# Joining the block inverses of two heads at once on four row groups of TensorE

## The chip, the cores and the metric

The kernel runs on one core of a Trainium2 chip. The core has TensorE (matrix products, here PE), VectorE (DVE), ScalarE (ACT), GpSimd (POOL), SyncE (SP, which here only issues transfers) and sixteen DMA engines. The metric is device time in microseconds, from the first to the last instruction. The profiler records one execution; its span is used to read where the time goes.

## The reference

The program is one transformer block with adaptive layer norms: a gated linear attention with a delta rule, then a feed-forward part whose hidden values are thinned two out of four. All data are fp32. The part that matters here is the recurrence of the attention, for 8 sequences of 256 tokens, 16 key heads with two value heads each, all of width 128:

```python
def step(S, inp):
    q_t, k_t, v_t, b_t, d_t = inp
    Sk = jnp.einsum('bhi,bhipj->bhpj', k_t, S)
    dv = b_t[..., None] * (v_t - Sk)
    upd = jnp.einsum('bhi,bhpj->bhipj', k_t, dv)
    S = S * d_t[:, :, None, :, None] + upd
    o = jnp.einsum('bhi,bhipj->bhpj', q_t, S)
    return (S, o)
```

Over a chunk of 128 tokens this is the solution of a triangular system. The kernel forms the triangular 128x128 matrix of each chunk, inverts it, and applies the inverse by matrix products.

## The kernel before, in words

The sequences are taken in four pairs, and the key heads in groups of four (`GH`), so that there are 16 groups and 64 turns of one "head" (a key head for a pair of sequences). A head has 8 triangular matrices: two sequences, two chunks, two value heads.

While one group is attended, the next is prepared in the background (`ahead`). `stage_a` projects and convolves the keys, makes the products of keys with decays (tile `a_t`) and writes the diagonal 32x32 blocks of each triangle to a scratch in DRAM. `stage_b` reads the 128 blocks of the group back with one block a partition, inverts them all at once on VectorE, and writes the inverses to DRAM in two orientations (`scr_x`, `scr_y`).

`levels` joins these inverses for one head. It reads the inverse blocks into `x_even`, `x_top` and the diagonal of `t_inv`, and then goes through four steps with a `yield` after each. Step one multiplies 32x32 blocks below the diagonal by inverse blocks (line 703, tile `ps_w`), and ScalarE copies the result (711, 712). Step two multiplies from the other side (line 717, `ps_t`); VectorE transposes one half (725) and ScalarE writes the joint 64x64 inverses to `t_inv` and `x_top` (729, 732, 738), of which a transfer moves a part to other partitions (730, `low_up`). Steps three and four do the same with 64x64 blocks (743 and 746, copy 750; 754 and 757, copies 760 and 761). In the 32-wide steps the blocks stand on partitions 0 to 31 and 64 to 95 (step one) or 32 to 63 and 96 to 127 (step two), so that successive products alternate between two of the array's four row groups. In the 64-wide steps they alternate between the two halves.

`attend` uses the finished inverse `t_inv` (lines 810 and 853) for one sequence of the head. There are two `t_inv` tiles: one is read for the head that is attended while the other is written for the next.

The main loop at the end goes through the heads. For each it makes a list of turns: the attention of two sequences, the join (`levels`) for the head that comes next, the projections for the next head, the output products of an earlier one. It takes one step of each turn in rotation, and after each rotation a measured amount of background work (`along`). This gives the order in which the program is written; a scheduler then places the instructions of each engine by its own estimates, so that the order within an engine is not quite that of the loop. All transfers are issued by SP and ACT; those of the joins are on SP, in order with the loads of decays (`dbc`), of the feed-forward weights (`w_ff`, `w_dn`) and the scratch traffic.

Of the kernel before, what the change touches and what calls it, by code (L numbers as in the profile page):

```python
# [18 lines left out]
P = 128  # L19
# [29 lines left out]
def adaln_block(  # L49
# [316 lines left out]
    with ExitStack() as scope:  # L366
# [45 lines left out]
        t_inv = [single.tile([P, 2 * NS, P], F32, name=f"t_inv{i}") for i in range(2)]  # L412
        x_top = single.tile([P, NS, 2 * Q], F32, name="x_top")
# [260 lines left out]
        def levels(rec, scr_x, scr_y, tt):  # L674

            hp = rec["hp"]
            xv = scr_x.rearrange("(g s q) a b -> g q a s b", g=GH, q=NQ)
            yv = scr_y.rearrange("(g s q) a b -> g q a s b", g=GH, q=NQ)
            a_f = rec["a"].rearrange("p i s t -> p (i s) t")
            NP = 2 * NS  # L680

            x_even = single.tile([P, NP, Q], F32, name="x_even")
            low_up = single.tile([P, NS, 2 * Q], F32, name="low_up")
            for q in (0, 2):
                nc.sync.dma_start(out=x_even[q * Q : (q + 1) * Q], in_=xv[hp, q])
            for q in (1, 3, 0, 2):
                rows = slice(q * Q, (q + 1) * Q)
                nc.sync.dma_start(out=tt[rows, :, rows], in_=yv[hp, q])  # L690
                if q < 2:
                    for i in range(2):
                        nc.sync.dma_start(
                            out=x_top[i * 2 * Q + q * Q : i * 2 * Q + (q + 1) * Q, :, rows],
                            in_=xv[hp, q, :, i * NS : (i + 1) * NS],
                        )
            nc.sync.dma_start(out=low_up[2 * Q :], in_=a_f[0 : 2 * Q, NS:, 2 * Q :])
            even = [slice(0, Q), slice(2 * Q, 3 * Q)]
            odd = [slice(Q, 2 * Q), slice(3 * Q, P)]
            ps = bank(ps_inv, [P, NP, Q], "ps_w")  # L700
            for s in range(NP):
                for h in range(2):
                    nc.tensor.matmul(
                        ps[odd[h], s, :],
                        lhsT=a_f[even[h], s, odd[h]],
                        rhs=x_even[even[h], s, :],
                        start=True,
                        stop=True,
                    )
            w1 = single.tile([P, NP, Q], F32, name="w1")  # L710
            nc.scalar.copy(w1[odd[0]], ps[odd[0]])
            nc.scalar.copy(w1[odd[1]], ps[odd[1]])
            yield
            ps = bank(ps_inv, [P, NP, Q], "ps_t")
            for s in range(NP):
                for h in range(2):
                    nc.tensor.matmul(
                        ps[even[h], s, :],
                        lhsT=w1[odd[h], s, :],
                        rhs=tt[odd[h], s, odd[h]],  # L720
                        start=True,
                        stop=True,
                    )
            low = mixp.tile([Q, NP, Q], F32, tag="low", name="low", bufs=1)
            nc.vector.transpose(
                low.rearrange("p s t -> p (s t)"),
                ps[even[0]].rearrange("p s t -> p (s t)"),
            )
            nc.scalar.activation(tt[even[1], :, odd[1]], ps[even[1]], AF.Copy, scale=-1.0)
            nc.sync.dma_start(out=low_up[0 : 2 * Q], in_=tt[2 * Q :, NS:, 2 * Q :])  # L730
            for i in range(2):
                nc.scalar.activation(
                    x_top[i * 2 * Q + Q : (i + 1) * 2 * Q, :, 0:Q],
                    low[:, i * NS : (i + 1) * NS],
                    AF.Copy,
                    scale=-1.0,
                )
            nc.scalar.activation(tt[even[0], :, odd[0]], ps[even[0]], AF.Copy, scale=-1.0)
            yield
            top, bottom = slice(0, 2 * Q), slice(2 * Q, P)  # L740
            ps = bank(ps_inv, [P, NS, 2 * Q], "ps_w2")
# [479 lines left out]
```

## Time and profile before

| | |
|---|---|
| three runs | 2126.72, 2133.49, 2134.71 us |
| median | 2133.49 us |
| span of the profiled execution | 2126.1 us |
| granted TensorE clock, mean | 0.988 |
| TensorE idle in the span | 72 us |
| 32-wide products, lines 703 and 717: records, busy | 4096, 102.0 us |
| 64-wide products, lines 743, 746, 754, 757: records, busy | 2048, 181.7 us |
| bytes moved over the span | 226.85 MB, mean 107 GB/s |

The profiled execution's own time is known by its span alone, which lies near the fastest of the three runs and 7.4 us below their median. "Busy" counts the time in which at least one record of a group is open; for short products on TensorE a record stays open far longer than it keeps the next from starting, so distances between starts say more. A line such as `L703 PE MATMUL ps_w<-x_even,a_t 32*32 32x32 f32 x2048 | 53.7, 194 | 7.0` gives the source line, the engine, the tile written and the tiles read, the shape, the number of records, the busy time in us, the mean of one record in ns, and the engine's idle time just before such records.

### The profile page before, as it was taken

Reading aid. Unit: us, or ns where it says so; the run is one execution under the profiler, and the core shown is the slowest. Engines: PE = TensorE matmul, PEld = TensorE weight load, DVE = VectorE, ACT = ScalarE, POOL = GpSimd, SP = SyncE. Lnnn points to the kernel's source line nnn. Section 1 sums busy time; section 2 is a strip of 40 time slices with the busy share of each in tenths; the row PEclk is TensorE's granted clock in tenths of the full one; section 3 lists DMA queues with packets and bytes.
Section 4 is the critical chain, followed back from the end, with each engine's and each line's share of the span. In section 5 each row is a group of like instructions: output and inputs, shape, how many; then the busy total and the mean of one; then the engine's idle time right before and its main releaser. Section 6 shows DMA issues by size and latency. Waiting matters only on the chain.

```text
span 2126.1 us, 46444 instructions
## 1 busy us (share of the span) xinstructions
PE 2054.1 (97%) x16684; PEld 1633.6 (77%) x16684; DVE 1660.8 (78%) x4039; ACT 1356.1 (64%) x4579; POOL 367.8 (17%) x375
## 2 busy tenths in 40 slices
PE   8989999999999999999999999999999999999998
PEld 5567777777777787778778687778778778787887
DVE  6788787878879587897878779787896958879357
ACT  3577767776766467576576666667666656666552
POOL 3121202112120111212021020211112011120010
PEclk9999999999999999999999999999999999999999
DMA  4342424233242443434343343443434244343236
GB/s 135 98 112 69 113 66 118 79 78 113 82 116 82 124 118 92 124 97 120 115 103 102 117 117 104 113 118 98 121 98 120 67 124 129 96 114 96 73 90 216
DMA packets 324517, 226.85 MB, mean 107 GB/s; under 512 B 254520, under 2 KB 266168, under 8 KB 324288
## 3 DMA queue, kind: packets, MB, share of 16 engines
q1 hardware_dynamic: 304416, 163.34, 28.8%
q10 hardware_dynamic: 19872, 60.54, 9.1%
q8 instruction: 133, 2.18, 0.4%
q14 instruction: 96, 0.79, 0.1%
HBM read 186.28 MB, written 29.12 MB: 101 GB/s over the span
## 4 chain that ended last, share of the span: by engine, by line
PE 66%; DVE 13%; DMA 7%; ACT 6%; issue 2%; SPq 1%; POOL 1%; ACTq 0%; DVEq 0%; POOLq 0%
PE ps_qv L432 10%; PE ps_y L907 9%; PE ps_z L646 8%; PE ps_ks L818 5%; PE ps_ff L190 4%; PE ps_k L432 3%; DVE cv L420 3%; PE ps_u L853 2%; PE ps_out L244 2%; PE ps_o L837 2%; PE ps_kk L532 2%; PE ps_gt L893 2%; PE ps_o L859 2%; DMA blk<-scr 2%; PE ps_u L810 2%
## 5 line engine op out<-in xcount | busy, mean ns | idle before, releaser
L420 DVE SCALAR_TENSOR_TENSOR cv<-ps_qv,conv_sb,cv 128x510 f32<-128x510 f32 (+1 forms) x564 | 410.0, 736 | 43.4 <-ACT cv L418 41.5
L432 PE MATMUL ps_qv<-h_bp,wh 128*128 128x512 f32 x768 | 367.3, 602 | 3.0 <-DVE cv L420 2.0
L105 POOL TENSOR_TENSOR rs<-ss,minus_halves 128x4 f32<-128x4 f32 x128 | 133.2, 1049 | 1040.8 <-DVE ss L864 1023.7
L646 PE MATMUL ps_z<-wh,h_bp 128*128 128x256 f32 x1024 | 249.9, 386 | 12.1 <-ACT gz L653 11.3
L907 PE MATMUL ps_y<-wo,og_p 128*128 128x256 f32 x1024 | 236.0, 380 | 0.9 <-DVE cv L420 0.9
L646 PEld LDWEIGHTS ps_z<-wh,h_bp 128*128 128x128 f32 x1024 | 186.3, 192 | 39.8 <-ACT gz L653 12.4
L432 PEld LDWEIGHTS ps_qv<-h_bp,wh 128*128 128x128 f32 x768 | 133.3, 192 | 105.4 <-issue 97.8
L418 ACT ACTIVATE cv<-ps_qv,conv_sb 128x512 f32<-128x512 f32 x188 | 129.3, 690 | 122.3 <-PE ps_qv L432 121.9
L907 PEld LDWEIGHTS ps_y<-wo,og_p 128*128 128x128 f32 x1024 | 188.0, 190 | 23.7 <-DVE cv L420 1.4
L604 DVE TENSOR_TENSOR tmp<-blk 128x30 f32<-128x30 f32 (+14 forms) x480 | 157.1, 327 | 46.8 <-DMA blk<-scr 37.6
L516 POOL TENSOR_TENSOR diag<-consts,bk 128x1032 f32<-128x1032 f32 x64 | 122.8, 1918 | 371.6 <-DVE bk L507 371.6
L844 ACT ACTIVATE junk<-o 128x128 f32<-128x128 f32 x512 | 154.1, 305 | 42.9 <-DVE o L860 36.4
L551 DVE TENSOR_TENSOR_SCAN e<-dbc,diag 128x1032 f32<-128x1032 f32 x60 | 137.9, 2299 | 47.6 <-POOL diag L516 46.3
L610 DVE TENSOR_TENSOR blk<-blk,tmp 128x30 f32<-128x30 f32 (+14 forms) x480 | 156.9, 327 | 9.6
L420 DVE SCALAR_TENSOR_TENSOR k_t<-ps_k,conv_sb,k_t 128x510 f32<-128x510 f32 (+1 forms) x189 | 139.2, 738 | 22.0 <-ACT k_t L418 20.3
L877 DVE SCALAR_TENSOR_TENSOR og<-o,rs,gz 128x128 f32<-128x128 f32 x512 | 143.9, 345 | 14.1 <-POOL rs L105 14.0
L818 PE MATMUL ps_ks<-u,cross 128*128 128x128 f32 x1024 | 144.7, 284 | 2.8 <-DVE aq L800 1.5
L784 ACT ACTIVATE vn<-ps_v,nk 128x256 f32<-128x256 f32 x256 | 105.7, 482 | 62.0 <-PE ps_v L779 61.2
L818 PEld LDWEIGHTS ps_ks<-u,cross 128*128 128x128 f32 x1024 | 133.7, 197 | 12.5 <-ACT u L812 5.3
L190 PE MATMUL ps_ff<-h,w_ff 128*128 128x128 f32 x1024 | 130.5, 277 | 3.3 <-ACT h L149 2.3
L190 PEld LDWEIGHTS ps_ff<-h,w_ff 128*128 128x128 f32 x1024 | 123.5, 192 | 10.8 <-issue 3.8
L432 PE MATMUL ps_k<-h_bp,wk 128*128 128x512 f32 x256 | 123.9, 609 | 2.0 <-ACT junk L451 1.2
(176 smaller groups left out, 4259.2 us busy)
## 6 DMA issues: line engine op xcount, KB each, us to landing
wh<-in_w_heads ACTq DMA_DIRECT2D x64, 640.0 KB, 4.1
w_ff<-in_w_ff SPq DMA_DIRECT2D x128, 256.0 KB, 3.0
dbc<-d_dram SPq DMA_DIRECT2D x60, 516.0 KB, 4.2
wo<-in_w_heads ACTq DMA_DIRECT2D x32, 512.0 KB, 3.7
w_dn<-in_w_down SPq DMA_DIRECT2D x64, 256.0 KB, 3.4
wk<-in_w_keys SPq DMA_DIRECT2D x16, 512.0 KB, 5.0
scr<-a_t SPq DMA_DIRECT2D x256, 32.0 KB, 2.4
blk<-scr SPq DMA_DIRECT2D x16, 512.0 KB, 3.7
```

What stands on the lines that cost most here:

```text
L105: nc.gpsimd.tensor_tensor(out=out, in0=in_, in1=minus_halves[:, :n], op=ALU.pow)
L190: nc.tensor.matmul(ps[:, a, l, :], lhsT=w[:, k, l, :], rhs=h2[:, k, :], start=(k == 0), stop=(k == CC - 1),)
L420: nc.vector.scalar_tensor_tensor(out=dst[:, :, d:], in0=ps[:, :, : T - d], scalar=taps[:, KC - 1 - d : KC - d], in1=dst[:, :, d:], op0=ALU ...
L432: nc.tensor.matmul(ps.rearrange("p b t -> p (b t)"), lhsT=w[k], rhs=h_bp[:, k, :], start=(k == 0), stop=(k == CC - 1),)
L551: nc.vector.tensor_tensor_scan(e.rearrange("p i s t -> p (i s t)"), dbc.rearrange("p i f -> p (i f)"), diag.rearrange("p s t -> p (s t)"), ...
L604: nc.vector.tensor_tensor(out=tmp, in0=blk[:, j, None, j + 1 :].to_broadcast([P, j, m]), in1=blk[:, 0:j, j, None].to_broadcast([P, j, m]), ...
L610: solved = nc.vector.tensor_tensor(out=blk[:, 0:j, j + 1 :], in0=blk[:, 0:j, j + 1 :], in1=tmp, op=ALU.subtract)
L646: nc.tensor.matmul(ps[:, n, :], lhsT=h_bp[:, k, i * T + n * P : i * T + (n + 1) * P], rhs=wh[:, k * 640 + 384 : (k + 1) * 640], start=(k = ...
L818: nc.tensor.matmul(ps_ks[:, ct, h, :], lhsT=cross[:, h, ct, :], rhs=u0[:, h, :], start=True, stop=True)
L844: nc.scalar.activation(junk, o[:, n, h, :], AF.Square, accum_out=ss[:, n, h : h + 1])
L877: nc.vector.scalar_tensor_tensor(out=og[:, n, h, :], in0=o[:, n, h, :], scalar=rs[:, 2 * n + h : 2 * n + h + 1], in1=gz[:, i, n, h, :], op ...
L907: nc.tensor.matmul(ps_y[:, n, :], lhsT=og_p[:, j // 2, i, n, j % 2, :], rhs=wo[:, j // 2, j % 2, :], start=(j == 0), stop=(j == 3),)
```

## The change

`levels` takes two heads (`pair`) and is called for every second head. Its 32-wide steps put the blocks of the second head on the row groups that the first one leaves free: `x_even` holds the first head's even blocks on row groups 0 and 2 and the second's on 1 and 3, and a new tile `moved` holds the second head's blocks below the diagonal and its odd inverse blocks, moved by 32 partitions by transfers. Successive products then go to four row groups. The 64-wide steps run over eight matrices a half instead of four, one head in each half. The minus signs move from the last copies into the copies between the steps, which take the whole tile in one instruction; VectorE transposes straight into `x_top`. There are three `t_inv`, since two heads' inverses are written while a third is read. To make room in SBUF the program asks for a smaller scratch for DMA descriptors.

```diff
-        t_inv = [single.tile([P, 2 * NS, P], F32, name=f"t_inv{i}") for i in range(2)]
-        x_top = single.tile([P, NS, 2 * Q], F32, name="x_top")
+        t_inv = [single.tile([P, 2 * NS, P], F32, name=f"t_inv{i}") for i in range(3)]
+        x_top = single.tile([P, 2 * NS, 2 * Q], F32, name="x_top")
...
-        def levels(rec, scr_x, scr_y, tt):
+        def levels(pair, scr_x, scr_y, tts):
...
+            for r in range(2):
+                for h in range(2):
+                    nc.sync.dma_start(out=x_even[rows(2 * h + r)], in_=xv[hp + r, 2 * h])
+            for h in range(2):
+                nc.sync.dma_start(out=moved[rows(2 * h + 1)], in_=a_f[1][rows(2 * h), :, rows(2 * h + 1)])
+            for q in (1, 3):
+                nc.sync.dma_start(out=tts[0][rows(q), :, rows(q)], in_=yv[hp, q])
+                nc.sync.dma_start(out=moved[rows(q - 1)], in_=yv[hp + 1, q])
+            for r in range(2):
+                for q in range(2):
+                    nc.sync.dma_start(out=x_top[rows(2 * r + q), :, rows(q)], in_=xv[hp + r, q])
+            for r, q in ((0, 2), (1, 2), (1, 3), (0, 0), (1, 0), (1, 1)):
+                nc.sync.dma_start(out=tts[r][rows(q), :, rows(q)], in_=yv[hp + r, q])
+            nc.sync.dma_start(out=low_up[rows(2, 2)], in_=a_f[1][rows(0, 2), :, rows(2, 2)])
...
             for s in range(NP):
                 for h in range(2):
+                    even, odd = rows(2 * h), rows(2 * h + 1)
                     nc.tensor.matmul(
-                        ps[odd[h], s, :],
-                        lhsT=a_f[even[h], s, odd[h]],
-                        rhs=x_even[even[h], s, :],
-                        start=True,
-                        stop=True,
+                        ps[odd, s, :], lhsT=a_f[0][even, s, odd], rhs=x_even[even, s, :], start=True, stop=True
+                    )
+                    nc.tensor.matmul(
+                        ps[even, s, :], lhsT=moved[odd, s, :], rhs=x_even[odd, s, :], start=True, stop=True
                     )
             w1 = single.tile([P, NP, Q], F32, name="w1")
-            nc.scalar.copy(w1[odd[0]], ps[odd[0]])
-            nc.scalar.copy(w1[odd[1]], ps[odd[1]])
+            nc.scalar.activation(w1, ps, AF.Copy, scale=-1.0)
             yield
...
+                    nc.tensor.matmul(
+                        ps[even, s, :], lhsT=w1[odd, s, :], rhs=tts[0][odd, s, odd], start=True, stop=True
                     )
+                    nc.tensor.matmul(
+                        ps[odd, s, :], lhsT=w1[even, s, :], rhs=moved[even, s, :], start=True, stop=True
+                    )
+            nc.scalar.copy(tts[1][rows(2), :, rows(3)], ps[rows(3)])
+            nc.sync.dma_start(out=low_up[rows(0, 2)], in_=tts[1][rows(2, 2), :, rows(2, 2)])
+            for r in range(2):
+                nc.vector.transpose(x_top[rows(2 * r + 1), :, rows(0)], ps[rows(r)])
+            nc.scalar.copy(tts[0][rows(2), :, rows(3)], ps[rows(2)])
+            for r in range(2):
+                nc.scalar.copy(tts[r][rows(0), :, rows(1)], ps[rows(r)])
+            yield
...
-                if not solved:
-                    for _ in levels(rec, *scratch, t_inv[head % 2]):
+                if head == 0:
+                    for _ in levels(recs[:2], *scratch, [t_inv[r] for r in range(2)]):
                         along()
...
                 if coming:
-                    solved = True
-                    turns.append(levels(coming[0], *coming[1], t_inv[(head + 1) % 2]))
+                    if hp % 2 == 1:
+                        turns.append(levels(coming[0], *coming[1], [t_inv[(head + r) % 3] for r in (1, 2)]))
...
-    nc = bacc.Bacc("TRN2", target_bir_lowering=False, num_devices=1)
+    nc = bacc.Bacc("TRN2", target_bir_lowering=False, num_devices=1, dynamic_dma_scratch_size=1024)
```

In the changed kernel the first 32-wide step is on lines 707 and 710, the second on 720 and 723, the 64-wide ones on 737, 740, 748 and 751.

## The prediction

> **What bounds the kernel now.** I read the page first: busy shares, the 40 slices, the chain that ended last.
>
> ```profile
> PE 2054.1 (97%) x16684; PEld 1633.6 (77%) x16684; DVE 1660.8 (78%) x4039; ACT 1356.1 (64%) x4579; POOL 367.8 (17%) x375
> ...
> PE   8989999999999999999999999999999999999998
> ...
> PEclk9999999999999999999999999999999999999999
> ...
> PE 66%; DVE 13%; DMA 7%; ACT 6%; issue 2%; SPq 1%; POOL 1%; ACTq 0%; DVEq 0%; POOLq 0%
> ```
>
> TensorE is busy in nine tenths or more of nearly every slice, at a constant granted clock, and idle for only 2126.1 - 2054.1 = 72 us. No other engine comes near. So time on TensorE is the currency: what the change takes from its stream leaves the end, less whatever new waiting takes its place. The groups by line and form give what the joins (levels) cost now:
>
> ```profile
> L703 PE MATMUL ps_w<-x_even,a_t 32*32 32x32 f32 x2048 | 53.7, 194 | 7.0 <-DMA x_even<-scr_x 6.9
> L717 PE MATMUL ps_t<-t_inv,w 32*32 32x32 f32 x2048 | 48.3, 193 | 2.5 <-DMA t_inv<-scr_y 1.2 <-ACT w L711 0.5 <-ACT junk L451 0.5
> L754 PE MATMUL ps_t<-t_inv,w 64*64 64x64 f32 x512 | 45.8, 229 | 2.0 <-ACT w L750 2.0
> L743 PE MATMUL ps_w<-x_top,a_t 64*64 64x64 f32 x512 | 45.4, 230 | 3.8 <-ACT x_top L732 2.5 <-DMA out<-res 1.3
> L729 ACT ACTIVATE t_inv<-ps_t 32x256 f32<-32x256 f32 x64 | 24.0, 374 | 42.4 <-DVE low L725 41.2
> L732 ACT ACTIVATE x_top<-low 32x128 f32<-32x128 f32 x128 | 39.4, 308 | 2.9
> ```
>
> The 32-wide products hold TensorE for 53.7 + 48.3 = 102.0 us. Each product of the program is two records here (1024 products, 2048 records a line). A record's 194 ns is mostly latency, so the cost must be read from the spacing of starts. That is in the timeline of one ordinary stretch:
>
> ```profile
> 602.21 0.58 PEld L717 LDWEIGHTS ps_t<-t_inv,w 32*32 32x32 f32 x32 [0.17 <-DVE cv L420]
> 602.21 0.69 PE L717 MATMUL ps_t<-t_inv,w 32*32 32x32 f32 x32
> 602.84 1.16 PE L810 MATMUL ps_u<-vn,t_inv 128*128 128x128 f32 x8
> 603.83 1.88 PE L432 MATMUL ps_qv<-h_bp,wh 128*128 128x512 f32 x4
> 608.61 0.83 PE L818 MATMUL ps_ks<-u,cross 128*128 128x128 f32 x6
> 609.37 0.27 PE L743 MATMUL ps_w<-x_top,a_t 64*64 64x64 f32 x1
> 609.83 0.22 PE L743 MATMUL ps_w<-x_top,a_t 64*64 64x64 f32 x1
> 609.98 0.66 PE L447 MATMUL ps_n2k<-consts,k_t 128*128 128x128 f32 x4
> ```
>
> Three prices come from it. (1) **Spacing of 32-wide records**: 32 records end 0.69 us after the first start; less the last one's 0.19, 0.50 us hold 31 steps, 16 ns each, 32 ns for the two squares of a pair. (2) **Are the two concurrent?** Four 128x512 records take 1.88 us; less 0.60 for the last, 1.28 / 3 = 427 ns for 512 columns, 0.83 ns a column, so 32 columns need 27 ns. Two in turn would need 54; they take 32. So two squares on two row groups do run side by side. (3) **Switching shape**: six 128x128 records end 0.83 us after 608.61; less 0.28 the last one starts at 609.17, and the first 64-wide one 0.20 us later, where 128x128 records follow each other at 0.83 - 0.28 = 0.55, / 5 = 0.11 us: 0.09 us on the way in. On the way out, the last 64-wide pair starts at 609.83 and the next product at 609.98, 0.15 us, where such pairs follow each other at (609.83 - 609.37) / 7 = 0.066 us or less: about 0.09 us. After the 32-wide group: 602.21 + 0.50 = 602.71 to 602.84, 0.13 us, of which 32 ns is the pair itself. Together 0.18 us for every unbroken stretch of small products.
>
> **The change, part by part.**
>
> *32-wide joins on four row groups.* The number of products stays: 64 a pair of heads, 4096 records in all. At 16 ns they cost 4096 x 0.016 = 65.5 us now. (Check: 102.0 us busy, less about 172 stretches x (0.194 - 0.016) us of latency tail = 71 us, waits included.) No row of before shows four squares at once. Best bound: a set of four takes what two take, 32 ns, saving half: -32.8 us. Zero bound: four take the time of two pairs. Worst bound: all four stream one after another, 4 x 27 = 108 ns instead of 2 x 32 = 64 for the same work, 1024 sets x 44 ns = +45 us. I take the best bound, because the nearest row is the pair, which runs side by side into one PSUM bank already; within a pair the second starts about 10 ns after the first or sooner (lines 743 and 746 start at 609.37 and 609.38, then at 609.59 and 609.60), so four starts fit into 32 ns.
>
> The Trainium skill speaks against it twice. "TensorE: Matmul & The Clock Gate", section "Wait — 56ns, not 53.3ns?", puts a floor of about 25 ns on the distance of any two starts; by it four would take 100 ns, and the term would be about 1024 x 36 ns = +37 us as an estimate. The measured 16 ns lies below that floor. "TensorEngine Tiling (Array Packing)", section "Gotcha 1: PSUM Pressure", says that different row tiles can't access one PSUM bank simultaneously; the pairs of line 703 do write one bank, and take 32 ns for what would need 54. Neither rule stands against its row, though no run here shows four.
>
> *Fewer stretches.* In the order of TensorE's instructions as the two programs are built, small products stand in 309 unbroken stretches before (172 of 32-wide, 137 of 64-wide) and 178 after (111 and 67): joint heads double the length of a stretch. 131 x 0.18 = -24 us. Lower bound 0.5 of it, where a stretch begins after a wait that hides the switch: -12.
>
> *64-wide joins* keep their products and already run as two squares side by side. 0.
>
> *ScalarE.* Before, per pair of heads: lines 711, 712 4 x 0.36, lines 729, 738 4 x 0.37, line 732 4 x 0.31, line 750 2 x 0.37, lines 760, 761 4 x 0.38 = 6.4 us. After: one 128x256 copy 0.37, four 32x256 copies 1.5, three copies of 512 columns at about 0.69 (line 418 reads 128x512 in 690 ns) 2.1 = 4.0 us. 32 x 2.4 = 77 us less ScalarE work. TensorE waited on ScalarE in small sums only, so I count 3 us of it: -3, bounds 0 and -15. DVE keeps 64 transposes of 32x256 (now straight into x_top, 430 ns): 0.
>
> *Transfers on SP.* 22 a pair instead of 24. But the first join of a pair now needs six of them (four x_even, two moved) where a head's needed two; an x_even issue holds SP's queue for 448 ns (median), so the sixth is 4 x 0.45 = 1.8 us later than the second was. Behind it on SP stand x_top, t_inv, low_up, and the dbc and w_ff loads. It matters where the blocks have only just been inverted: the first pair of each of the 16 groups. There TensorE waits for x_even already, 8.8 + 6.9 us in total. Bounds: 0 (other products stand before the join and cover it) and 16 x 1.8 = +29. The order after puts other products between the third and fourth of these in places, which covers part: +10. The other 16 pairs read blocks that have long been written: 0. Low_up's later half waits one transfer of 2.2 us as before, half as often: 0.
>
> *Start.* Two heads must be joined ahead of the first attend: one more set of 64-wide pairs in two stages, 2 x 8 x 0.066 = 1 us, and a few issues: +2.
>
> *The rest.* A third t_inv and a doubled x_top are cleared by POOL in the first microseconds, long before 85 us: 0. The DMA scratch is no matter where all issues come from SP and ACT queues. The third t_inv keeps writes of a pair off the buffer being read; the bank pool gets four requests a pair for eight: 0.
>
> Sum: -32.8 - 24 - 3 + 10 + 2 = -48 us. Since TensorE, now idle for 3.4% of the span, will wait a little more on DVE (78%, unchanged) I keep -45. Against the profiled span of 2126.1 us: 2081. The three runs have 2126.7 to 2134.7, median 2133.5, 7 us above the span; from the median, **2088 us**.
>
> **Rivals.**
>
> *Four squares are no faster than two pairs* (the zero bound: instruction supply, or the bank). Then -45 + 33 = -12 to -24 with all switches saved: 2110 to 2121. For: no row shows 128 small instructions in one stretch. Against: starts 5 to 10 ns apart.
>
> *The time is given back in waits.* Even heads have no joins left to fill TensorE with while attend waits for ScalarE and DVE; chains of a joint pair are longer. If waits grow from 72 us of idle time by 25 to 30: about 2115. For: DVE is on 13% of the chain. Against: 77 us less ScalarE work, and background projections everywhere.
>
> *Slower: the four squares go one after another.* Place: the 1024 sets of lines 707/710 and 720/723. Price: 108 ns a set instead of 64, +45, against the rest of the sum, -45 + 33 = -12: +33, so 2166. The kernel becomes slower from the point where a set takes more than 64 + 12 / 1.024 = 76 ns. For: no row shows four. Against: the pairs.
>
> **How the numbers follow.** Forecast 0.66 (2065 to 2105); no faster than pairs 0.12; given back in waits 0.15; slower 0.07. A change within 0.5% (10.7 us, 2122.8 to 2144.2) is about what a measurement here cannot tell from none. The first two and most of the third lie below 2122.8: faster 0.87, same 0.06, slower 0.07. The range runs from the full stream and ScalarE terms without new waits (-32.8 - 24 - 15 = -72) to the first two rivals: 2062 to 2120; the slower one and tails stay out.
>
> **What would show it.** Right: 32-wide records at about 8 ns spacing, so lines 707 to 723 together near 32 us of spacing; TensorE busy about 2000; idle time before ps_w on DMA under 30 us; ScalarE busy near 1280. Wrong: 16 ns spacing (first rival), 27 ns (slower), or idle time before attend's lines well above 72 us (second).

## The result, and the profile after

The changed kernel takes **2259.3 us** (median of four runs, 2254.9 to 2263.2), the kernel before 2130.1 in the same comparison: ratio 1.061, 95% interval 1.058 to 1.064. The forecast was 2088, so the direction was wrong.

The page of the changed kernel, the lines that answer to those shown of before:

```profile
PE 2039.8 (91%) x16684; PEld 1621.1 (72%) x16684; DVE 1642.3 (73%) x4039; ACT 1278.2 (57%) x4265; POOL 373.0 (17%) x376
...
PE   8889998999898798999999799898999969899898
...
PEclk9999999999899899999999899999999989999899
...
PE 38%; DVE 25%; DMA 13%; ACT 4%; issue 3%; SPq 2%; POOL 2%; POOLq 0%; DVEq 0%; ACTq 0%
```

The span is 2252.9 us. TensorE's row, solid before, now has a dip every few slices, and the clock row has dips too. On the chain, TensorE falls from 66% to 38% and VectorE rises from 13% to 25%. Three numbers account for the 126.8 us between the two spans (the split of the clock from each profile's mean granted clock, 0.988 before and 0.966 after, which counts idle time as well, so it is an estimate):

| us | before | after | difference |
|---|---|---|---|
| TensorE idle (span less busy) | 72.0 | 213.1 | +141 |
| lost to the slower clock, (1 - clock) x span | 25.5 | 76.6 | +51 |
| TensorE's work at full clock (the rest) | 2028.6 | 1963.2 | -65 |

So TensorE did get 65 us less to do, a little more than the 57 that the stream and switch terms came to. All of it, and another 127 us, went into waiting and a slower clock. The groups by line and form of the changed kernel, for the joins:

```profile
L751 PE MATMUL ps_t<-low_up,w 64*64 64x64 f32 x512 | 43.5, 245 | 28.5 <-DMA low_up<-t_inv 28.5
...
L707 PE MATMUL ps_w<-x_even,a_t 32*32 32x32 f32 x1024 | 36.2, 199 | 11.0 <-DMA x_even<-scr_x 9.3 <-DVE a_t L563 1.6
L710 PE MATMUL ps_w<-x_even,moved 32*32 32x32 f32 x1024 | 34.0, 199 | 13.2 <-DMA x_even<-scr_x 13.0
...
L729 DVE STREAM_TRANSPOSE x_top<-ps_t 32x256 f32<-32x256 f32 x64 | 28.4, 443 | 33.5 <-ACT t_inv L726 31.9
...
L720 PE MATMUL ps_t<-t_inv,w 32*32 32x32 f32 x1024 | 26.6, 200 | 1.6 <-DMA t_inv<-scr_y 1.1 <-ACT w L714 0.5
L723 PE MATMUL ps_t<-moved,w 32*32 32x32 f32 x1024 | 26.5, 200 | 1.2 <-DMA moved<-scr_y 1.2
```

Lines 707 and 710 overlap, so their busy times can't be added. The distance of starts is read from one unbroken run of `ps_t` (windows view of the changed kernel for the tile `ps_t` alone; the columns are the window, its length, then busy time and records of TensorE and of its weight loads, VectorE, ScalarE, the granted clock, DMA share, GB/s):

```profile
1048.98:1049.76 0.78, 0.75 (x64) 0.64 (x64) 0.00 (x0) 0.00 (x0) 1.00 0.26 53
```

64 records are open for 0.75 us; less 0.19 for the last, 0.56 us hold 63 steps, **8.9 ns** each, where before had a median of 16.2. Four squares do run side by side, into one bank. The Trainium skill says otherwise in "TensorE: Matmul & The Clock Gate", section "Wait — 56ns, not 53.3ns?", which puts a floor of about 25 ns between starts; the 8.9 ns here decide against it for squares on different row groups.

And the longest waits of TensorE in the changed kernel (in all, how often, the longest, us):

```profile
PE ps_t L751 <- DMA low_up<-t_inv: 28.5, 13, 4.4
PE ps_h L147 <- DVE xn L137: 26.0, 4, 8.3
PE ps_ff L190 <- DMA w_ff<-in_w_ff: 14.6, 10, 3.0
PE ps_w L710 <- DMA x_even<-scr_x: 13.0, 8, 3.9
PE ps_z L646 <- DVE cv L420: 11.5, 9, 1.6
...
PE ps_w L707 <- DMA x_even<-scr_x: 9.3, 6, 2.9
```

`x_even` and `low_up` belong to the join; `xn` and `w_ff` belong to the feed-forward part, which the change doesn't touch. A list like this names what came last, not what was late first.

### The profile page after: what moved, and what is told of

Its sections match the earlier page's. It is cut to its first block, busy times and chain, and to the rows that moved or that the text cites. A ratio compares the mean times of both kernels' runs of the same rounds, so it can differ in the third digit from the quotient of the medians.

```text
span 2252.9 us, 45807 instructions
## 1 busy us (share of the span) xinstructions
PE 2039.8 (91%) x16684; PEld 1621.1 (72%) x16684; DVE 1642.3 (73%) x4039; ACT 1278.2 (57%) x4265; POOL 373.0 (17%) x376
## 4 chain that ended last, share of the span: by engine, by line
PE 38%; DVE 25%; DMA 13%; ACT 4%; issue 3%; SPq 2%; POOL 2%; POOLq 0%; DVEq 0%; ACTq 0%
DVE cv L420 7%; PE ps_y L901 7%; PE ps_qv L432 5%; PE ps_z L646 4%; PE ps_ks L812 3%; DVE e L551 2%; PE ps_ff L190 2%; DMA blk<-scr 2%; DMA low_up<-t_inv 2%; PE ps_k L432 2%; DVE tmp L604 2%; DVE blk L610 2%; DVE k_t L420 2%; DMA scr<-a_t 2%; DVE a_t L563 2%
## 5 line engine op out<-in xcount | busy, mean ns | idle before, releaser
L420 DVE SCALAR_TENSOR_TENSOR cv<-ps_qv,conv_sb,cv 128x510 f32<-128x510 f32 (+1 forms) x564 | 410.2, 738 | 22.8 <-ACT cv L418 20.5
L901 PE MATMUL ps_y<-wo,og_p 128*128 128x256 f32 x1024 | 243.1, 386 | 9.9 <-issue 8.2
L646 PEld LDWEIGHTS ps_z<-wh,h_bp 128*128 128x128 f32 x1024 | 191.8, 195 | 66.3 <-ACT junk L451 16.1
L551 DVE TENSOR_TENSOR_SCAN e<-dbc,diag 128x1032 f32<-128x1032 f32 x60 | 138.2, 2303 | 50.6 <-POOL diag L516 46.5
L871 DVE SCALAR_TENSOR_TENSOR og<-o,rs,gz 128x128 f32<-128x128 f32 x512 | 145.1, 345 | 19.9 <-POOL rs L105 19.6
L563 DVE TENSOR_TENSOR a_t<-ps_kk,e 128x512 f32<-128x512 f32 x128 | 82.1, 683 | 101.0 <-PE ps_kk L532 96.0
L190 PE MATMUL ps_ff<-h,w_ff 128*128 128x128 f32 x1024 | 136.7, 280 | 19.3 <-DMA w_ff<-in_w_ff 14.6
L653 ACT ACTIVATE gz<-ps_z 128x512 f32<-128x512 f32 x128 | 76.0, 597 | 99.6 <-PE ps_z L646 96.1
```

The costliest lines, as they stand in the source:

```text
L190: nc.tensor.matmul(ps[:, a, l, :], lhsT=w[:, k, l, :], rhs=h2[:, k, :], start=(k == 0), stop=(k == CC - 1),)
L420: nc.vector.scalar_tensor_tensor(out=dst[:, :, d:], in0=ps[:, :, : T - d], scalar=taps[:, KC - 1 - d : KC - d], in1=dst[:, :, d:], op0=ALU ...
L551: nc.vector.tensor_tensor_scan(e.rearrange("p i s t -> p (i s t)"), dbc.rearrange("p i f -> p (i f)"), diag.rearrange("p s t -> p (s t)"), ...
L646: nc.tensor.matmul(ps[:, n, :], lhsT=h_bp[:, k, i * T + n * P : i * T + (n + 1) * P], rhs=wh[:, k * 640 + 384 : (k + 1) * 640], start=(k = ...
L871: nc.vector.scalar_tensor_tensor(out=og[:, n, h, :], in0=o[:, n, h, :], scalar=rs[:, 2 * n + h : 2 * n + h + 1], in1=gz[:, i, n, h, :], op ...
L901: nc.tensor.matmul(ps_y[:, n, :], lhsT=og_p[:, j // 2, i, n, j % 2, :], rhs=wo[:, j // 2, j % 2, :], start=(j == 0), stop=(j == 3),)
```

## Where in a group the time is lost

A group has four heads' turns. Measured from one head's first `ps_kq` to the next one's, the means over the program are, for the turn of the first to the fourth head: 39.3, 33.3, 29.2, 23.6 us before and 49.8, 35.0, 23.8, 24.7 after. TensorE's idle time in the first grows from 1.4 to 8.7 us. The first turn alone grows by 10.5 us, more than the four together (7.9 us); the third, in which no join is left, gets shorter.

The inversion of the next group's blocks on VectorE starts with the third turn and ends with the fourth. The windows view of one group shows it, from the first to the last step of that inversion, and from there to the first `ps_u` of the next group (here and below the columns are: window, length, busy time and records of TensorE, weight loads, VectorE, ScalarE, GpSimd, granted clock, DMA share, GB/s). Before:

```profile
1278.60:1324.20 45.60, 44.86 (x292) 35.29 (x291) 43.91 (x125) 27.59 (x86) 4.02 (x5) 1.00 0.26 82
1324.20:1344.10 19.90, 19.87 (x209) 14.28 (x207) 17.06 (x35) 16.00 (x52) 5.35 (x5) 1.00 0.44 120
```

After:

```profile
1352.40:1405.20 52.80, 50.54 (x275) 39.58 (x274) 50.63 (x145) 32.82 (x112) 5.50 (x8) 1.00 0.24 70
1405.20:1428.50 23.30, 17.71 (x247) 13.00 (x247) 12.66 (x23) 10.80 (x31) 4.33 (x4) 0.91 0.56 140
```

In the first stretch VectorE is full in both kernels (43.9 of 45.6, 50.6 of 52.8 us), and TensorE no less (44.9 and 50.5 us). That VectorE sets how long the inversion takes after the change is tested below (after_short_inv). It holds 20 more instructions there than before. The inversion's own are the same: the same first stretch for the tile `blk` alone (TensorE has none; the columns are VectorE, ScalarE, GpSimd), before and then after:

```profile
1278.60:1324.20 45.60, 19.58 (x60) 1.72 (x2) 0.14 (x1) 1.00 0.26 82
```

```profile
1352.40:1405.20 52.80, 19.50 (x60) 1.75 (x2) 0.15 (x1) 1.00 0.24 70
```

What came in is other work, for instance on the keys of the group after (tile `k_t`; TensorE, weight loads, VectorE, ScalarE), before and then after:

```profile
1278.60:1324.20 45.60, 2.08 (x12) 1.97 (x12) 0.00 (x0) 0.00 (x0) 1.00 0.26 82
```

```profile
1352.40:1405.20 52.80, 5.32 (x31) 4.81 (x32) 3.77 (x6) 1.38 (x2) 1.00 0.24 70
```

And for the joins' second steps (tile `ps_t`, the same columns) in this stretch, before and then after:

```profile
1278.60:1324.20 45.60, 1.38 (x48) 1.13 (x48) 0.43 (x1) 1.50 (x4) 1.00 0.26 82
```

```profile
1352.40:1405.20 52.80, 0.00 (x0) 0.00 (x0) 0.00 (x0) 0.00 (x0) 1.00 0.24 70
```

TensorE has 48 records before, with one VectorE instruction of 0.43 us, and none after. So a join is TensorE work that asks next to nothing of VectorE. Before, it filled TensorE in the third turn while VectorE inverted. After, the third turn has none; projections, gates and convolutions stand in its place, each of which hands VectorE something to do, and in VectorE's order that stands ahead of steps of the inversion. The inversion ends later, TensorE has by then done what else there was, and waits (second stretch: busy 17.7 of 23.3 us, clock 0.91).

That is **theory "cover"**. Means over the 15 groups after the first, us, for the kernels below (here the inversion is counted to the end of the ScalarE copy to `xb` that follows VectorE's last step, on average some 1.5 to 1.8 us later than in the stretches above; VectorE's records are counted whole where they start inside, so parts can exceed the whole):

| | before | after | late_pair | again | inv_first_late | all_one |
|---|---|---|---|---|---|---|
| inversion, first to last step | 47.1 | 52.7 | 52.8 | 48.8 | 45.2 | 46.7 |
| VectorE in it: the inversion | 19.6 | 19.5 | 19.9 | 19.7 | 19.7 | 19.6 |
| VectorE in it: other work | 31.8 | 40.2 | 40.5 | 34.1 | 31.5 | 31.8 |
| from there to the first `ps_u` | 19.3 | 22.7 | 19.3 | 22.0 | 22.7 | 19.0 |
| of it TensorE busy | 18.4 | 16.5 | 14.8 | 20.2 | 20.5 | 18.5 |
| from there to the next inversion | 58.7 | 58.0 | 60.8 | 58.4 | 58.3 | 58.6 |

After less before is +5.6, +3.4 and -0.7, 8.3 us a group; fifteen groups make 125 of the 127 us. The +3.4 is not the inversion's own: it stays in again and inv_first_late (22.0 and 22.7), which also join the first two heads as a pair, and is not there in late_pair (19.3), which joins them singly. But in those two TensorE is busy for 20.2 and 20.5 us of it, instead of 16.5.

## The experiments

Times are medians; ratios are to the kernel before, run on the same chip, with 95% intervals.

### Is it the array?

**two_groups**: the changed kernel with its four-square loops split (the second step likewise), so that only two row groups are in use at a time.

```diff
             for s in range(NP):
                 for h in range(2):
                     even, odd = rows(2 * h), rows(2 * h + 1)
                     nc.tensor.matmul(
                         ps[odd, s, :], lhsT=a_f[0][even, s, odd], rhs=x_even[even, s, :], start=True, stop=True
                     )
+            for s in range(NP):
+                for h in range(2):
+                    even, odd = rows(2 * h), rows(2 * h + 1)
                     nc.tensor.matmul(
                         ps[even, s, :], lhsT=moved[odd, s, :], rhs=x_even[odd, s, :], start=True, stop=True
                     )
```

> The changed kernel, but each 32-wide step runs the first head's squares and then the second's, so that two squares are in the array at once instead of four; transfers, tiles and copies are those of the change. Spacing of the 32-wide records should go from about 7 ns back to 16 ns, 4096 x 9 ns = 37 us more on TensorE. Theory 'edge' (the time of the changed kernel is lost where a group of heads begins: the joint pair's transfers and steps follow directly on the inversion, and TensorE has nothing else left): most of those 37 us fall where TensorE waits anyhow, 2255 to 2280 us. Rival 'array' (the four squares themselves are what is slow): faster than the changed kernel, below 2230. Rival 'TensorE still bounds': 2259 + 37 = 2296.

Measured: 2268.4 us, 1.066 (1.064 to 1.069). Records 14.5 ns apart instead of 8.9. By the ratios it costs some 12 us more than four squares, so the four squares are worth something and are not the loss.

**before_one_square**: the kernel before with `for s` and `for h` exchanged, so that one square is used at a time.

> The kernel before, but each 32-wide step runs all squares of one row group and then all of the other, so that one square is in the array at a time: spacing from 16 ns to about 27 to 31 ns, 4096 x 11 to 15 = 45 to 61 us more on TensorE, spread evenly over all turns. If TensorE's stream sets the end throughout: 2175 to 2190 us. Theory 'cover' (VectorE is full in the inversion phase, TensorE 97% busy): TensorE is tight there, so most of it shows, 2150 to 2190; that a saving does not show and a cost does is what is to be tested.

Measured: 2157.4 us, 1.013 (1.010 to 1.016). Records 29.1 ns apart: 4096 x (29.1 - 16.2) = 53 us more stream by this estimate (TensorE's busy time grows by 2090.4 - 2054.1 = 36), of which about 27 arrive in the time. Even in the kernel before, TensorE time is not paid in full: by these two figures at a half to three quarters.

### Is it the pairs, or where they stand?

Here the kernel keeps everything of the change (three `t_inv`, smaller DMA scratch) but has the old single join beside the new one, and chooses per turn `hp`; the edit of late_pair:

```diff
-                    if hp % 2 == 1:
+                    if hp == 1:
                         turns.append(levels(coming[0], *coming[1], [t_inv[(head + r) % 3] for r in (1, 2)]))
+                    elif hp != 2:
+                        turns.append(one_level(coming[0][0], *coming[1], t_inv[(head + 1) % 3]))
```

`all_one` takes the single join in each turn. `mid_pair` pairs the second and third head (in turn 0; turn 1 has no join). `edge_pair` pairs the first two heads of a group in the turn that ends the group before (turn 0 has none). `late_pair` pairs the third and fourth head, so that the third turn (2) has none.

> The changed kernel's frame (three t_inv, tiles of twice the width, smaller scratch), but every head is joined alone, with the code of before, one head ahead. Theories 'edge' and 'uneven': as the kernel before, 2120 to 2145 us. Rival 'frame': 2200 or more.

> The changed kernel, but only the second and third head of a group are joined as a pair; the first head of a group (whose blocks have only just been inverted) and the fourth are joined alone, with the code of before. Half of the pairs' savings remain. Theory 'edge': the loss at the beginning of a group goes, and about half of the saved TensorE work (64 us by the busy times and clock) shows: 2085 to 2125 us. Rival 'uneven' (pairs make the turns uneven wherever they stand: some turns have two heads' joins, some none): half of the loss stays, about 2195. Rival 'frame' (third t_inv, wider tiles, smaller scratch cost it): about 2250.

> The complement: only the first and second head of a group are joined as a pair, the third and fourth alone. Theory 'edge': the whole loss stays and half of the saving goes: 2250 to 2290 us. Rival 'uneven': half of the loss, about 2195. Rival 'frame': about 2250 as well; the kernel before this one tells it apart.

> One pair per group again: the third and fourth head are joined as a pair in the second head's turn, the first and second alone, so that the third head's turn holds no join, and the beginning of a group is as before. Theory 'cover': the next group's blocks are inverted on VectorE in the turns of the third and fourth head; joins are TensorE work that asks almost nothing of VectorE and fill TensorE there; without one, other work comes forward, its VectorE part goes ahead of the inversion, which then ends about 5.6 us later (47 to 52.7 us in the traces), and TensorE runs dry after it. So this one should lose what the two other single pairs did not: about 15 x 5.6 = 84 us less some saved work, 2175 to 2205 us. Rival 'number of pairs' (each pair costs something, the second more): 2130 to 2140, as the other two.

| | us | ratio |
|---|---|---|
| all_one | 2119.0 | 0.995 (0.993 to 0.998) |
| mid_pair | 2133.1 | 1.004 (1.002 to 1.005) |
| edge_pair | 2137.1 | 1.005 (1.003 to 1.007) |
| late_pair | 2251.1 | 1.058 (1.054 to 1.062) |

The parts around the pairs cost nothing (all_one). The pair at a group's edge, which I had suspected first because its join waits for fresh inverses, costs 18 us over all_one. So "edge" (2250 to 2290 for edge_pair) and "uneven" (about 2195 for either) both missed. Taking the join out of the third turn alone costs 132, nearly the whole, and more than "cover" had priced (2175 to 2205): against before, the inversion's 5.7 us a group make 86 us, and another 2.1 us a group (31 us) come behind it, before the next inversion, which "cover" does not explain. The same two stretches of late_pair read like those of the changed kernel, with the same VectorE time (50.7) in the first:

```profile
1345.80:1399.80 54.00, 50.26 (x271) 39.33 (x272) 50.74 (x145) 32.75 (x112) 5.50 (x8) 1.00 0.21 64
1399.80:1422.50 22.70, 19.06 (x207) 13.60 (x206) 12.10 (x22) 11.15 (x34) 4.33 (x4) 0.80 0.52 131
```

### Is it the cover?

**again** puts work into the changed kernel that nothing needs: a single join of the fourth head in the third turn, though the pair has joined it already (1536 more records).

```diff
+                    if hp == 2:
+                        turns.append(one_level(coming[0][0], *coming[1], t_inv[(head + 1) % 3]))
```

> The changed kernel with work added: in the third head's turn the fourth head is joined a second time, alone, with the same result. It adds 64 matmul records of 32 wide and 32 of 64 wide, 9 ScalarE copies and one transpose per group. Theory 'cover': TensorE is filled again while VectorE inverts, other work stays behind, the inversion takes 47 us again: faster than the changed kernel although it does more, 2150 to 2200 us. Rivals 'TensorE bounds' and 'number of pairs': slower than the changed kernel by up to 16 x 3 = 48 us, 2260 to 2310.

Measured: 2201.0 us, 1.034 (1.031 to 1.037): **58 us faster with more to do**. The rivals' 2260 to 2310 are out, but it is only part of the loss, at the upper end of what "cover" gave (2150 to 2200). In the table, the inversion falls to 48.8 us and VectorE's other work in it to 34.1. Its stretches, VectorE 46.3 us and 132 instructions in the first:

```profile
1322.20:1370.80 48.60, 47.34 (x314) 38.12 (x313) 46.28 (x132) 29.78 (x94) 4.66 (x7) 1.00 0.26 77
1370.80:1394.60 23.80, 21.83 (x276) 15.76 (x276) 18.76 (x38) 15.79 (x50) 5.16 (x5) 1.00 0.58 141
```

**before_short_inv, after_short_inv** leave out 15 of the 30 elimination steps in both kernels, so the inverses are not the true ones:

```diff
-            for j in range(1, Q - 1):
+            for j in range(2, Q - 1, 2):
```

> The kernel before with the same steps of the inversion left out. Theory 'cover': there TensorE is busy for 45.6 of the 47.1 us of the phase, so VectorE's 9.8 us save little: 2090 to 2120 us, a much smaller gain than in the changed kernel. If VectorE sets the length in both, the gain is the same in both: about 2000.

> The changed kernel, of whose block inversion every other elimination step is left out (15 of 30; the inverses are not those of the reference). VectorE has about 9.8 us less per group, all in the inversion phase. Theory 'cover': VectorE sets the length of that phase in the changed kernel, so it ends up to 9.8 us earlier in 15 groups: 2259 - 110 to 147, 2110 to 2150 us. Rival 'the joint chain after the inversion is too long' alone: the phase moves but the wait after it stays, 2200 or more.

Measured: 2120.5 us, 0.996 (0.994 to 0.998), and 2082.5 us, 0.979 (0.976 to 0.982). Both lose some 120 us of VectorE work. The kernel before gains 9 us by it, the changed one 177, more than "cover" gave (2110 to 2150). So VectorE's time in the inversion is worth next to nothing before the change, when TensorE has as much to do there, and all of it and more after. And with the shorter inversion the change is worth 2082.5 - 2120.5 = -38 us, near the forecast's -45: TensorE idles for 2079.5 - 1997.6 = 82 us, near the 72 of before. The pages of before_short_inv and after_short_inv:

```profile
PE 2058.4 (97%) x16684; PEld 1627.1 (77%) x16684; DVE 1534.2 (72%) x3559; ACT 1371.0 (65%) x4581; POOL 372.4 (18%) x375
```

```profile
PE 1997.6 (96%) x16684; PEld 1585.6 (76%) x16684; DVE 1523.7 (73%) x3559; ACT 1282.6 (62%) x4264; POOL 376.0 (18%) x376
```

### Is it the order?

**inv_first** leaves the work as it is and binds the order: what a group's turns issue is placed behind the last step of the inversion that this group waits for. **inv_first_late** also binds the fifth and later rotations of the last head to what of the next inversion has been written by then (the edit shown; in inv_first, `behind` is `held`).

```diff
+            held = last[0]
...
                 while turns:
-                    with tc.issue_after(first_solved) if head == 0 else ExitStack():
+                    behind = last[0] if hp == GH - 1 and turn >= 4 else held
+                    with tc.issue_after(behind):
                         turns = [t for t in turns if next(t, turns) is not turns]
-                    along()
+                        along()
+                    turn += 1
```

> The changed kernel with VectorE's order alone changed: what the loop traces for a group (its attentions, the next group's keys, the feed-forward) is queued on VectorE behind the last step of that group's own inversion. No work is added or removed. Counted in the built order and priced by the rows, the other VectorE work between the first and last step of the inversion falls from 37.7 to 29.0 us a group (before: 29.3). Theory 'cover': it is that work, come forward, which delays the inversion; with it behind, the phase is back at about 47 us and TensorE has work left after it: 2090 to 2170 us. Rival 'the joins must fill TensorE at that place' in the narrow sense, order being no matter: no more than 30 us better than the changed kernel, above 2229.

> As the one before, and the late steps of the fourth head's turns (from the fifth rotation on) are queued on VectorE behind the next group's inversion as well (28.6 us of other work in the phase). Theory 'cover': the same or up to 20 us better.

> The same order on the kernel that joins every head alone in the changed frame (2119 us). There the other work in the phase falls only from 29.2 to 27.1 us. Theory 'cover': within 25 us of 2119, either way; if the order alone were a gain in itself, as much as in the changed kernel, far below 2060.

Measured: 2155.0 (1.011; 1.009 to 1.014), 2144.9 (1.006; 1.004 to 1.009) and, for the same order with single joins, 2127.3 (0.999; 0.997 to 1.001). The order alone takes back 104 and 114 us of the changed kernel's loss, and does not help single joins (2119.0 without it). It is not VectorE's order alone, though: the bind is on VectorE, but in inv_first_late 12323 of TensorE's 16684 records and 2349 of ScalarE's 4265 stand at the same place in their order as in the changed kernel, so the scheduler moved work on those engines too. The stretches of inv_first_late:

```profile
1288.00:1332.00 44.00, 42.67 (x237) 34.58 (x238) 42.84 (x123) 27.28 (x92) 4.25 (x6) 1.00 0.27 79
1332.00:1357.40 25.40, 21.78 (x278) 15.33 (x276) 21.41 (x45) 16.68 (x51) 5.68 (x6) 1.00 0.50 122
```

VectorE holds 123 instructions in the first, as before the change (125). TensorE's idle time falls from 213 to 141 us, and the granted clock rises from 0.966 to 0.986. The waits for `low_up` fall from 28.5 to 5.8 us and for `x_even` from 22.3 to 3.6, without a transfer changed, so they went with the order:

```profile
PE ps_t L751 <- DMA low_up<-t_inv: 5.8, 2, 3.6
...
PE ps_w L707 <- DMA x_even<-scr_x: 3.2, 3, 1.6
...
PE ps_w L710 <- DMA x_even<-scr_x: 0.4, 2, 0.3
```

**late_pair_ifl, mid_pair_ifl**: the same order on the kernels with one pair a group.

> The kernel with one pair (third and fourth head) that lost 122 us, with VectorE's order of inv_first_late. Theory 'cover': its loss goes as that of the changed kernel did. Theory 'head of a group' for what is left: its chain after the inversion is as before, so it ends better than the changed kernel in the same order (2145): 2105 to 2130 us. If the missing joins in the third head's turn cost something beyond the order: 2145 or more.

> One pair (second and third head) in the first head's turn, with the order of inv_first_late; without that order it took 2133. Other VectorE work in the phase falls from 29.0 to 25.2 us. Theory 'head of a group' has nothing to lose here: 2100 to 2133 us.

Measured: 2143.1 (1.007; 1.005 to 1.010) and 2127.5 (1.000; 0.998 to 1.002). The pair in the middle now costs nothing, and gains nothing. The late pair stays some 16 us dearer than single joins in the same order (forecast 2105 to 2130), so what is left is not the edge's pair, as I had thought it might be.

### What keeps the rest?

With the order right, TensorE has less to do than in all_one and still the time is 26 us longer (18 us longer than single joins in the same order, 2127.3). One wait stands out in inv_first_late (waits view, then the timeline of TensorE around one of the three):

```profile
PE ps_h L147 <- DVE xn L137: 24.5, 3, 8.3
```

```profile
1222.30 1.13 PE L244 MATMUL ps_out<-w_dn,hid 128*128 128x256 f32 x4 [1.83 <-DMA w_dn<-in_w_down]
1231.76 0.69 PE L147 MATMUL ps_h<-consts,xn 128*128 128x128 f32 x2 [8.33 <-DVE xn L137]
1232.24 1.91 PE L812 MATMUL ps_ks<-u,cross 128*128 128x128 f32 x8
```

In the built order of the changed kernel no product stands between the last `ps_out` of one feed-forward unit and the first `ps_h` of the next, at three places; before, 56 stood there. TensorE waits 8 us for store, sum and norm while `ps_ks` is queued behind. **inv_first_late_ff**, **after_ff** and **all_one_ff** start the second unit of each pair of sequences three steps later:

```diff
                 units[0] = later(units[0])
+                units[1] = later(units[1], 3)
```

> The kernel with the background held behind the inversion (2145 us, some 26 us above the kernel that joins single heads, 2119), and the second feed-forward unit of each pair of sequences begins three steps later. Theory, queue: three times in this program the transposes ps_h of the next unit stand directly behind the last ps_out in TensorE's order (no product between them; 56 in the kernel before), and TensorE waits 8 us each time for the chain of store, sum and norm behind xn, 24.5 us in all, and then runs at half clock for 10 us each, another 15 us. With 38 products between them the wait goes: 2105 to 2122, the wait of ps_h on xn below 4 us. Rival, VectorE: what is left is VectorE's load and not this wait; the idle time turns up elsewhere: 2138 to 2150.

> The changed kernel with the second feed-forward unit three steps later and nothing else. Theory, queue: the 26 us of waiting of ps_h on xn and half of the slow clock behind it go, 26 to 40 us: 2220 to 2234; the late inversion of the blocks stays. Rival, VectorE: 2250 to 2262.

> The kernel that joins every head by itself (2119 us), with the same delay of the second unit. It has 39 products between ps_out and ps_h already and waits 2.7 us there, so either theory expects no change: 2114 to 2124.

Measured: 2132.9 (1.002; 1.001 to 1.004), 2243.1 (1.054; 1.052 to 1.056), 2129.4 (1.002; 1.000 to 1.003). By the ratios -9, -15 and +14 us. The wait went (1.0 us left in inv_first_late_ff), yet all three forecasts were missed: the control wasn't to change and lost 14, so the delay itself costs something. Under the same delay, pairs and single joins are now 3.5 us apart, within their intervals, instead of 26.

But TensorE's idle time is still 2130.0 - 2006.5 = 124 us against 73 in all_one_ff, and now names the weights: `w_dn` 15.4 us, `w_ff` 12.1, together 0.5 before:

```profile
PE ps_out L244 <- DMA w_dn<-in_w_down: 15.4, 6, 3.5
...
PE ps_ff L190 <- DMA w_ff<-in_w_ff: 12.1, 10, 2.6
```

**ifl_ff_w4** gives them a fourth buffer:

```diff
-... feed_forward(feed_pool, 2 * bp + j // NCH, j % NCH, ya) ...
+... feed_forward(feed_pool, 2 * bp + j // NCH, j % NCH, ya, 4) ...
```

> The kernel with the inversion first and the later second unit (2133 us, 1.0023 of the kernel before), with four buffers instead of three for the weights of the feed-forward part. There TensorE waits 15.4 us for w_dn and 12.1 us for w_ff (0.5 us in the kernel before): a joint pair of heads issues up to ten transfers in a row on SP ahead of such a load. Theory, SP: a fourth buffer lets a load be issued one product earlier, ahead of that burst; of the 27 us at least half go and the time falls by 8 to 20 us, 2112 to 2125. Rival, VectorE or the rest: the loads keep their places behind the burst or other waits take over: 2128 to 2138.

Measured: 2134.7 us, 1.004 (1.002 to 1.005). The waits for weights are gone altogether, and the time hasn't moved. The new list's head:

```profile
PE ps_u L847 <- ACT o L826: 19.6, 8, 6.0
PE ps_n2q L447 <- DVE cv L420: 12.8, 5, 4.2
```

Idle time is 2134.5 - 2010.0 = 124.5 us, as much as it was. So the late weights weren't the cause: with these waits gone, waits for other things add up to the same idle time.

## Why the prediction was wrong, step by step

- **The step that failed** is the first: "time on TensorE is the currency: what the change takes from its stream leaves the end, less whatever new waiting takes its place". A share of 97% over the span hid a stretch of some 47 us in each group in which VectorE is as full as TensorE (43.9 of 45.6 us) and in which the end of VectorE's work is what the next group's joins wait for. There TensorE's joins were cover: taking them out of the third turn let other work in that goes through VectorE, and from then on VectorE's time was the currency (half of the inversion's steps are worth 9 us before and 177 after). The sum put the new waiting at 10 us for `x_even` and 3 us for VectorE; the runs showed 141 us of idle time and, by the estimate, 51 us of slower clock, against 65 us of work saved. I read VectorE's 78% over the span, and no window.
- **Four squares**: right. 4096 x (16.2 - 8.9) = 30 us, forecast 32.8. **Fewer stretches**: in line as far as can be seen. Stream and switches together were put at 57, TensorE's work fell by 65; the two were not measured apart.
- **ScalarE**: 1278 us busy, forecast near 1280; it bought nothing that can be seen.
- **The signs of being right** were the wrong ones to look at: 8.9 ns (about 8), 22.3 us of waiting for `x_even` (under 30) and ScalarE's 1278 us were all met in a kernel 127 us slower. Only TensorE's busy time (2039.8 against about 2000) was not. None of them looks at VectorE.
- **Transfers on SP**: +10 forecast for `x_even`; its wait grew by 22.3 - 6.9 = 15.4 (the prediction's 8.8 + 6.9 us of waiting before are one wait, seen by the weight loads and by the products). `low_up`, forecast 0, grew from 1.0 to 28.5. Both go with the order (3.6 and 5.8 in inv_first_late), so SP's six issues alone don't make these waits.
- **The second rival** said "Even heads have no joins left to fill TensorE with", which is the place. It was priced at 25 to 30 us of idle time; measured are 141, and 51 us of slower clock that I had no term for. What its pricing lacked is that the scheduler fills the gap, with work that goes through VectorE. The prediction counted stretches of small products in TensorE's built order, and didn't look at what VectorE's order holds between two steps of the inversion.
- **The third rival** (four squares one after another) fell with the 8.9 ns.

**Shown**: the loss comes from the third turn's missing join (late_pair), goes partly with a join put back there (again), goes with less VectorE work in the inversion (after_short_inv), and 114 of some 130 us go with the order alone (inv_first_late). **Only argued, or open**: what is left to the forecast in that order, 2144.9 against 2088; why the scheduler brings that work forward, since its estimates can't be seen; and why the 65 us of TensorE time that were saved show in none of the kernels with the full inversion. TensorE's idle time is 124 us with and without the waits for weights, and falls to 82 us with half of the inversion's steps; that agrees with a phase that VectorE paces. But after_short_inv also lacks the 8 us waits of `ps_h`, so the two are not told apart there.

The fastest of the kernels with the full inversion is all_one, 0.995 of before: the change without its pairs. I did not take that gain apart.

## What to carry to other kernels

Before you price an edit by the busiest engine, cut the span into the program's phases and look which engine is full in each and whose end is waited for; work on another engine may be cover, and here the cover that was taken away was refilled with work for the fuller engine. If a scheduler places the work, compare the order on the *other* engines' queues, above all on the one that is full in that phase. A wait named in the list is worth its time only if nothing else is due at that moment: here 27 us of named waits were removed and the time stayed.

## What the runs showed of the hardware

- 32-wide fp32 records start 29.1 ns apart on one square, 14.5 to 16.2 on two row groups, 8.9 on four, into one PSUM bank.
- In the changed kernel idle time of TensorE is paid twice: by the estimate above, 51 of the 127 us are time at half clock. Short gaps can be enough: in the kernel before, eight of the nine half-clock stretches begin within 4 us of the start of an idle gap of 1.0 to 2.7 us (the ninth lies at the program's end). But not every such gap is followed by one; the gap of 2.2 us at 1704.0 was not. An idle gap of 2.6 us that began at 1023.0 ran into this window (columns as in the stretches above; the clock is 0.50):

```profile
1025.30:1028.70 3.40, 3.16 (x8) 2.54 (x9) 3.40 (x9) 1.21 (x5) 0.00 (x0) 0.50 0.02 5
```

The Trainium skill, "TensorE: Matmul & The Clock Gate", section "HAM oscillation — how this bites in real kernels", gives idle gaps over about 3.4 us as what brings the clock down. This trace agrees that gaps go ahead of the slower clock, but the kernel before has no gap longer than 2.71 us and still nine stretches at half clock, of 3.4 to 10.2 us.
